# Opening layer 1 with four streams of q and k, and the last row of layer 0 by halves of channels

## The chip, the cores and the metric

The kernel runs on one core of one Trainium2 chip. The metric is the device time of one execution in microseconds (us). A core has five engines that run side by side, each through its own queue of instructions in order: PE (TensorE, matrix products), DVE (VectorE), ACT (ScalarE), POOL (GpSimd) and SP (SyncE, which here only issues transfers). They wait for one another by semaphores. PE writes its results into PSUM, which has eight banks; ACT and DVE bring them from there into SBUF, the working memory.

## The reference, cut to what matters

The input x has 128 rows of 256 positions with 256 channels. Two layers follow each other; each normalises over groups of channels, applies attention along each row and adds the input back.

```python
# layer 0: gated attention with 8 heads and a bias from pair_repr
x = x + _L0_conv_ref(_gn(x), ...)
# layer 1: banded attention with 4 heads
x = x + _L1_conv_ref(_gn(x), ..., 16)

def _gn(v, G=32, eps=1e-5):
    g = v.reshape(B_, H_, W_, G, C_ // G)
    m = jnp.mean(g, axis=(1, 2, 4), keepdims=True)
    s = jnp.var(g, axis=(1, 2, 4), keepdims=True)
    return ((g - m) / jnp.sqrt(s + eps)).reshape(v.shape)

def _L1_conv_ref(x, w_in, b_in, w_out, b_out, band):
    qkv = x2 @ w_in.T + b_in
    q, k, v = jnp.split(qkv, 3, axis=-1)          # 4 heads of 64
    scores = jnp.einsum('bhid,bhjd->bhij', q, k) / jnp.sqrt(D)
    scores = jnp.where(jnp.abs(i - j) <= band, scores, -jnp.inf)
    attn = jax.nn.softmax(scores, axis=-1)
    out = jnp.einsum('bhij,bhjd->bhid', attn, v)
    return out @ w_out.T + b_out
```

The statistics of `_gn` run over all rows. Layer 1 cannot begin before the last row of layer 0 has been added up and measured.

## The kernel before, in words

All data is float32. A row lies in SBUF with channels on the 128 partitions, in two halves of channels, and 256 positions along the free axis. Layer 1 works on pairs of rows: pair i has the rows 2i and 2i + 1, and there are 64 pairs. Between the layers the rows go through DRAM: layer 0 stores them with `settle` and its DMA at L1062, layer 1 loads them again with `load1` (L792, tiles `yg`).

The order of nearly all instructions is written out by hand (`tc.manual_schedule`), so on each engine they run in the order in which the Python code issues them. Layer 1 takes POOL into this order too; before it, and in what stands ahead of its `manual_schedule` block, POOL is placed by the framework.

*The end of layer 0.* `plain_output` is the output product of a row (32 matrix instructions in the trace, L587, tile `po`), `finish` (L1052) adds the row's input on DVE and `settle` (L1060) takes `bn_stats` of each half of channels. `settle_pair` does the same for the two rows of `o_last`. Then `channel_columns` joins the statistics: `bn_aggr` (L304), a product `ps_m` (L310), four small DVE instructions, a product `ps_v` (L319), a root on ACT (L322) and `rstd` (L324). Between these PE runs filler products with the tile `warm` (`keep_on`, L1261): five, two and three of them. `least` (L998) is a minimum that only a last test needs.

*Layer 1.* `normal(i)` normalises a pair into `1xn`, by DVE (L1309) or, for all pairs from 2 on, by ACT (L1307, with `shift` from L1554), and POOL forms three sums of it (`row_sums`, L579 to L581, tile `1ts`). q, k and the output are each a `Summed` stream: a 2x2 product done with seven products in place of eight, in the order 2, 1, 5, 6, 7, 4, 3. They accumulate in one PSUM bank, and after each the stream's half of the bank is taken out by ACT (2, 5, 6, 4) or DVE (1, 7, 3). `in_turn` runs several streams side by side, product by product. `values(s)` is v of one row (L1346, tile `p1v`, copied by ACT at L1353); `scores(s)` is the banded q k (L1367), the exp on ACT (L1375), and on POOL the mask (L1377, tile `1p`) and a sum (L1384). `attend(i)` is the weighted sum over v (L1408, tile `1av`) and the sums of weights (L1420, `1zs`). Their reciprocals `rz` (L1445) go out to DRAM and come back spread over the partitions (`by_transfer`, L1453 and L1457, tile `near`), and `divide` (L1477) reads `1av` and writes `1at`, which the output stream `1o` takes.

PSUM in layer 1: a ring of four banks serves streams, values and scores; `1av` and `1zs` have two banks each and one buffer. The loop over pairs in the steady state is: scores of pair i, `finish(i - 3)`, `attend(i - 1)`, `sums`, a stretch of three streams (q and k of pair i + 1, output of pair i - 2), `normal(i + 2)`, `divide(i - 1)`, values of pair i + 1. In the first two stretches and in the third there is no output stream yet, so only two streams run side by side:

```python
normal(0, False)
for p in weights:
    nc.gpsimd.memset(p, 0.0)
values(0)
values(1)
normal(1, False)
nc.vector.scalar_tensor_tensor(shift1, mean1, -1.0, rstd1, op0=ALU.mult, op1=ALU.mult)
stretch(0, -1)
```

Of the kernel before, what the change touches and what calls it, by code (L numbers as in the profile page):

```python
# [9 lines left out]
F32 = mybir.dt.float32  # L10
AF = mybir.ActivationFunctionType
ALU = mybir.AluOpType
# [3 lines left out]
P = 128  # L16
R = 256
# [22 lines left out]
def conv_preact_kernel(  # L40
# [35 lines left out]
    def proj_bank(name):  # L76
        return bank("proj", name)
# [591 lines left out]
    class Summed(Seven):  # L669
# [2 lines left out]

        def __init__(self, pool, weights, x, t, name, tag, bias=None, y=None):
            self.weights, self.x, self.t, self.by_token, self.name = weights, x, t, False, name
            self.bias, self.y = bias, y
            self.to = pool.tile([P, 4, R], F32, tag=tag, name=name, bufs=1)
            self.mid = pool.tile([P, R], F32, tag=f"mid{tag}", name=f"mid{name}", bufs=1)

        def out(self, to, half, m, r):

# [89 lines left out]
    with ExitStack() as both:  # L772
# [22 lines left out]
        with ExitStack() as lay0:  # L795
# [280 lines left out]
            def settle_pair(i):  # L1076

                if i >= 0:
                    settle(2 * i, 2 * i % XG, 2 * i % XG + 1, i)


            with tc.manual_schedule(
# [166 lines left out]
                weighted(S - 1)  # L1249
                gated(S - 1)  # L1250
                plain_output(S - 2)
                settle_pair(last - 1)
                finish(S - 2)
                plain_output(S - 1)
                finish(S - 1)
                warm = proj_bank("warm")

                def keep_on(n):
# [1 line left out]
                    for _ in range(n):  # L1260
                        nc.tensor.matmul(warm[:, 0, :], lhsT=ident, rhs=out_sb[:, 0, :], start=True, stop=True)  # L1261
# [8 lines left out]
        with ExitStack() as lay:  # L1270
# [10 lines left out]
            nc.gpsimd.memset(place, 0.0)  # L1281
            for half in range(2):
                nc.gpsimd.memset(place[KB * half : KB * (half + 1), 16 * half : 16 * (half + 1)], 1.0)

            spread = att.tile([P, 2, 2, P], F32, name="spread", bufs=1)
            for half in range(2):
                for r in range(2):
                    nc.gpsimd.tensor_copy(  # L1288
                        spread[:, half, r].rearrange("p (j d) -> p j d", j=2),
                        ident[:, B * r + 16 * half :: D1].unsqueeze(2).to_broadcast([P, 2, D1]),  # L1290
                    )
            xns, tss = {}, {}

            shift1 = att.tile([P, 2], F32, name="shift1", bufs=1)
# [1 line left out]
            def normal(i, by_scalar):  # L1296

                if 2 * i >= S:
                    return
                load1(i + 1)  # L1300
                xns[i] = row.tile([P, 4, R], F32, tag="xn", name=f"1xn{i}", bufs=2)
                for r in range(2):
                    for half in range(2):
# [16 lines left out]

            ats, ats_t, outputs, last_ots = {}, {}, {}, {}

            def stretch(i, j, amid=lambda n: None):


                streams = [
                    Summed(row, quarters1[w], xns[i], tss[i], f"1{w}{i}", w, bias=bqk[:, 0:2] if w == "q" else None)
                    for w in "qk"
                ]
                f, g = streams  # L1330
# [3 lines left out]
                in_turn(streams, amid)  # L1334
                for r in range(2):
                    st[2 * i + r].update(q=f.to[:, 2 * r : 2 * r + 2, :], k=g.to[:, 2 * r : 2 * r + 2, :])

            def values(s):
                if s >= S:
                    return  # L1340
                i, r = divmod(s, 2)
                ps = proj_bank(f"p1v{s}").rearrange("p a (b c) -> p (a b) c", c=P)
                for b in range(NB):
                    for kt in range(2):
                        for half in range(2):
                            nc.tensor.matmul(  # L1346
                                ps[KB * half : KB * (half + 1), b, :],
                                lhsT=xns[i][:, 2 * r + kt, KB * b : KB * (b + 1)],
                                rhs=w_in_t[:, kt, 2 * C + P * half : 2 * C + P * (half + 1)],
                                start=(kt == 0), stop=(kt == 1),  # L1350
                            )
                v = row.tile([P, NB, P], F32, tag="v", name=f"1v{s}")
                nc.scalar.copy(v, ps)  # L1353
                st[s]["v"] = v

            def scores(s, engine=nc.gpsimd):
                q, k = st[s]["q"], st[s]["k"]
# [186 lines left out]
            with tc.manual_schedule(engines={  # L1544
                mybir.EngineType.PE, mybir.EngineType.Activation, mybir.EngineType.DVE, mybir.EngineType.Pool,
                mybir.EngineType.SP,
            }):
                normal(0, False)
# [5 lines left out]
                nc.vector.scalar_tensor_tensor(shift1, mean1, -1.0, rstd1, op0=ALU.mult, op1=ALU.mult)  # L1554
                stretch(0, -1)
                last = S // 2 - 1
                for i in range(last):
                    s = 2 * i
                    scores(s)
                    scores(s + 1)  # L1560
                    finish(i - 3)
                    attend(i - 1)
                    sums(i - 1)
                    inverse(i - 1, 0)

                    def amid(n):
# [12 lines left out]
                    values(s + 3)  # L1579

                def all_of(s):
                    for _ in project(s):
# [241 lines left out]
```

## Time and profile before

| what | us |
|---|---|
| median of 3 runs | 3093.72 |
| lowest and highest run | 3090.98 and 3093.94 |
| the profiled execution, its own time | 3092.16 |
| span of the profiled execution, first to last instruction | 3090.2 |
| last row's output product begins on PE | 2012.46 |
| first product of layer 1 on PE | 2020.01 |
| third pair's streams begin (`1xn` of pair 2) | 2049.86 |
| first stretch with three streams begins | 2065.39 |

Times inside the execution count from the start of its span. The mean granted clock of PE was 0.993. A line of a timeline has the start, the length, the engine, the line of the kernel, the operation, what it writes and reads, its shape and how many were merged; in brackets stands how long the engine was idle before it and what ended that. Matrix instructions are pipelined, so their lengths overlap; prices are therefore taken from start to start.

### The profile page before, as it was taken

Reading aid. Unit: us, or ns where it says so; the run is one execution under the profiler, and the core shown is the slowest. Engines: PE = TensorE matmul, PEld = TensorE weight load, DVE = VectorE, ACT = ScalarE, POOL = GpSimd, SP = SyncE. Lnnn points to the kernel's source line nnn. Section 1 sums busy time; section 2 is a strip of 40 time slices with the busy share of each in tenths; the row PEclk is TensorE's granted clock in tenths of the full one; section 3 lists DMA queues with packets and bytes.
Section 4 is the critical chain, followed back from the end, with each engine's and each line's share of the span. In section 5 each row is a group of like instructions: output and inputs, shape, how many; then the busy total and the mean of one; then the engine's idle time right before and its main releaser. Section 6 shows DMA issues by size and latency. Waiting matters only on the chain.

```text
span 3090.2 us, 142498 instructions
## 1 busy us (share of the span) xinstructions
PE 3004.1 (97%) x62701; PEld 2061.0 (67%) x62701; DVE 2251.8 (73%) x4506; ACT 1911.6 (62%) x4323; POOL 1903.1 (62%) x1913
## 2 busy tenths in 40 slices
PE   6879999999999999999999999999999999999997
PEld 4546666666666666666666666667777777777775
DVE  4677788778877877787878787746666666666665
ACT  4656666666666666666666666645555555555553
POOL 3045656566666666666666665566777667777674
PEclk9999999999999999999999999999999999999999
DMA  9942222222222222222222222224444444444443
GB/s 378 423 136 53 53 65 62 57 56 65 62 57 56 65 62 53 60 65 62 52 62 65 62 52 61 65 57 100 103 97 100 104 99 98 98 105 98 99 97 71
DMA packets 385413, 280.84 MB, mean 91 GB/s; under 512 B 285104, under 2 KB 354192, under 8 KB 378640
## 3 DMA queue, kind: packets, MB, share of 16 engines
q1 hardware_dynamic: 383888, 269.27, 33.1%
q8 instruction: 494, 8.09, 1.1%
q0 software_dynamic: 752, 2.36, 0.2%
q14 instruction: 135, 1.11, 0.1%
q10 hardware_dynamic: 144, 0.00, 0.0%
HBM read 202.38 MB, written 69.17 MB: 88 GB/s over the span
## 4 chain that ended last, share of the span: by engine, by line
PE 91%; DMA 4%; DVE 2%; POOL 1%; ACT 0%; issue 0%; SPq 0%; DVEq 0%; POOLq 0%; ACTq 0%
PE sim L836 9%; PE av L868 7%; PE p1v L1346 7%; PE p1q L587 7%; PE po L587 6%; PE pbv L932 6%; PE p1k L587 6%; PE p1o L587 6%; PE pv L587 6%; PE pq L587 6%; PE pk L587 5%; PE pg L587 5%; PE zs L881 4%; DMA pr<-in_L_conv_pair_repr_dram 4%; PE 1sim L1367 3%; PE 1av L1408 3%
## 5 line engine op out<-in xcount | busy, mean ns | idle before, releaser
L849 ACT ACTIVATE ex<-sim 128x512 f32<-128x512 f32 x1024 | 555.2, 606 | 253.1 <-PE sim L836 253.1
L858 DVE TENSOR_TENSOR both<-ex 128x512 f32<-128x512 f32 x508 | 445.8, 897 | 63.6 <-ACT ex L849 63.4
L631 POOL TENSOR_TENSOR v<-v,midv 128x512 f32<-128x512 f32 x64 | 82.1, 1283 | 453.7 <-ACT v L625 453.7
L836 PE MATMUL sim<-q,k 32*64 32x256 f32 x8192 | 289.4, 388 | 1.3 <-ACT ex L849 1.3
L961 DVE RECIPROCAL rz<-zs 128x256 f32<-128x256 f32 x128 | 225.0, 1758 | 67.8 <-PE zs L881 52.4
L868 PE MATMUL av<-ex,v 128*32 128x256 f32 x4096 | 244.6, 379 | 1.6 <-DVE at L1026 1.6
L691 ACT ACTIVATE 1q<-p1q,bqk 128x256 f32<-128x256 f32 x192 | 90.9, 473 | 240.7 <-PE p1q L587 122.4
L1377 POOL TENSOR_TENSOR 1p<-1ex,seen 128x768 f32<-128x768 f32 x127 | 231.4, 1822 | 11.8 <-ACT 1ex L1375 11.8
L1346 PE MATMUL p1v<-w_in_t,1xn 128*64 128x128 f32 x4096 | 236.3, 273 | 0.2 <-POOL spread L1288 0.2
L1346 PEld LDWEIGHTS p1v<-w_in_t,1xn 128*64 128x64 f32 x4096 | 231.5, 137 | 6.1 <-POOL place L1281 0.6
L579 POOL TENSOR_TENSOR 1ts<-1xn 128x512 f32<-128x512 f32 x64 | 81.4, 1272 | 239.0 <-ACT 1xn L1307 239.0
L836 PEld LDWEIGHTS sim<-q,k 32*64 32x64 f32 x8192 | 152.1, 131 | 113.6 <-issue 66.6
L631 POOL TENSOR_TENSOR q<-q,midq 128x512 f32<-128x512 f32 x64 | 82.0, 1282 | 195.4 <-ACT q L625 195.4
L868 PEld LDWEIGHTS av<-ex,v 128*32 128x32 f32 x4096 | 131.9, 110 | 78.8 <-DVE at L1026 2.1
L1477 DVE TENSOR_TENSOR 1at<-1av,1near 128x512 f32<-128x512 f32 x128 | 82.5, 686 | 128.0 <-DMA 1near<-rz_far 106.8
L1384 POOL TENSOR_TENSOR 1zp<-1p 128x512 f32<-128x512 f32 x127 | 162.3, 1278 | 10.0
L1353 ACT COPY 1v<-p1v 128x512 f32<-128x512 f32 x128 | 75.0, 586 | 125.0 <-PE p1v L1346 125.0
L343 DVE BATCH_NORM_STATS2 stats<-xs 128x6 f32<-128x128 f32 x512 | 100.2, 274 | 64.4 <-DMA xs<-in_x_dram 64.4
L881 PE MATMUL zs<-both,place 128*32 128x256 f32 x2032 | 137.5, 387 | 0.5 <-DVE both L858 0.5
L1025 DVE TENSOR_TENSOR av<-av,bv 128x512 f32<-128x512 f32 x125 | 87.4, 699 | 62.7 <-ACT bv L954 60.4
L1445 DVE RECIPROCAL 1rz<-1z 128x64 f32<-128x64 f32 (+1 forms) x192 | 129.8, 678 | 2.2
L685 DVE SCALAR_TENSOR_TENSOR 1o<-p1o,bo_v,yg 128x256 f32<-128x256 f32 x183 | 88.6, 484 | 56.4 <-PE p1o L587 53.7
(353 smaller groups left out, 8351.3 us busy)
## 6 DMA issues: line engine op xcount, KB each, us to landing
pr<-in_L_conv_pair_repr_dram SPq DMA_DIRECT2D x32, 1024.0 KB
xs<-in_x_dram SPq DMA_DIRECT2D x16, 2048.0 KB
yg<-x SPq DMA_DIRECT2D x64, 512.0 KB
out_dram<-1o SPq DMA_DIRECT2D x256, 128.0 KB
xg<-in_x_dram SPq DMA_DIRECT2D x252, 128.0 KB
x<-o SPq DMA_DIRECT2D x63, 512.0 KB
near<-rz_far SPq DMA_DIRECT2D x500, 64.0 KB
1near<-rz_far SPq DMA_DIRECT2D x124, 256.0 KB
```

Source lines behind the costliest of these rows:

```text
L587: nc.tensor.matmul(out[cols], lhsT=lhsT[:, cols], rhs=rhs, **flags)
L631: nc.gpsimd.tensor_tensor(self.to[:, 2:4], self.to[:, 2:4], self.mid, ALU.add)
L836: nc.tensor.matmul(sims[j][KB * c : KB * (c + 1), kt, :], lhsT=k[p0 : p0 + D0, 2 * r + half, k0 : k0 + KB], rhs=q[p0 : p0 + D0, 2 * r + ha ...
L849: nc.scalar.activation(ex[:, j], sims[j], AF.Exp, scale=1.0 / math.sqrt(D0))
L858: engine.tensor_tensor(both[:, j : j + 2], ex[:, j : j + 2, 0, :], ex[:, j : j + 2, 1, :], ALU.add)
L868: nc.tensor.matmul(to[D0 * j : D0 * (j + 1), half, :], lhsT=v[:, 2 * r + half, c0 : c0 + D0], rhs=weights(4 * half + j, kt), start=(kt == ...
L881: nc.tensor.matmul(zs[strip(j), 0, :], lhsT=place0[:, half, :], rhs=both[:, j, :], start=(half == 0), stop=(half == 1),)
L932: nc.tensor.matmul(ps[strip(j), acc, half, :], lhsT=stationary[n][:, half, strip(j)], rhs=bias_of[n][:, 4 * half + j, :], start=(n <= 2 an ...
L961: nc.vector.reciprocal(rz, zs[:, 0, :])
L1346: nc.tensor.matmul(ps[KB * half : KB * (half + 1), b, :], lhsT=xns[i][:, 2 * r + kt, KB * b : KB * (b + 1)], rhs=w_in_t[:, kt, 2 * C + P * ...
L1377: engine.tensor_tensor(p.rearrange("p j (r c) -> p (j r) c", c=WROW)[:, :, 0 : 2 * WSTEP] .rearrange("p r (t c) -> p r t c", c=WSTEP)[:, : ...
L1384: engine.tensor_tensor(zp, p[:, :, 0:R], p[:, :, R : 2 * R], ALU.add)
```

## The change

It touches the last row of layer 0 and the first three stretches of layer 1. The work done is the same.

- The statistics of the two rows of `o_last` (`settle_pair(last - 1)`) are issued before the last row is weighted and gated, not after it.
- The last row's output product is written into two banks, one for each half of channels, and the input is added and measured half by half. Its store is issued here.
- `least(S - 1)` is issued inside `channel_columns`, ahead of the copy of `mean`.
- `shift` is formed directly after `rstd`. Pair 0 is normalised by DVE, pair 1 by ACT; the second half of the channels comes first. The memsets of the weights, `place` and `spread` are issued on POOL after both pairs' row sums (`fill`).
- q and k of pairs 0 and 1 run as four streams in one `in_turn`. Pair 1's streams write into the tags of `out` and `at`, their intermediate tiles into `z` and `rz`.
- Then come the scores of rows 0 and 1, the values of rows 0 and 1, `normal(2)`, the values of rows 2 and 3, the scores of rows 2 and 3 and `attend(0)`. In the stretch of pair 2 the values of rows 4 and 5 are placed between its products, in eight pieces. From the stretch of pair 3 on the order is that of before.

```diff
-    def in_turn(sevens, amid=lambda n: None):
+    def in_turn(sevens, amid=lambda n: None, between=iter(())):
         for p in sevens:
             p.open()
             p.product(2, p.ps[:, 1, :], first=True)
             p.take(2)
+        next(between, None)
         for n in (1, 5, 6, 7, 4, 3):
             for p in sevens:
                 p.product(n)
                 p.take(n)
             if n in (1, 5):
                 amid(n)
+            next(between, None)
+        for _ in between:
+            pass
...
                 products(av, S - 1, lambda h, kt: ex1[:, h % 4, kt, :], range(1, 2))
+                settle_pair(last - 1)
                 keep_av(S - 1)
...
                 plain_output(S - 2)
-                settle_pair(last - 1)
                 finish(S - 2)
-                plain_output(S - 1)
-                finish(S - 1)
+                po = {}
+                for m in range(2):
+                    po[m] = proj_bank(f"po{S - 1}_{m}")
+                    for kt in range(2):
+                        in_columns(
+                            po[m][:, m, :], out_sb[:, kt, m * P : (m + 1) * P], st[S - 1]["at"][:, kt, :], B,
+                            start=(kt == 0), stop=(kt == 1),
+                        )
+                o = outs[last]
+                for m in range(2):
+                    nc.vector.tensor_tensor(o[:, 1, m, :], po[m][:, m, :], st[S - 1]["xt"][:, m, :], ALU.add)
+                    nc.vector.bn_stats(out=stats1[:, m, most1.entry(last + 1), :], in_=o[:, 1, m, :])
+                nc.sync.dma_start(out=rows(x1, last * XG, XG), in_=o)
...
-                mean1, rstd1 = channel_columns(st1, most1, 1, keep_on)
-                least(S - 1)
+                def meanwhile(n):
+                    if n == 5:
+                        least(S - 1)
+                    keep_on(n)
+
+                mean1, rstd1 = channel_columns(st1, most1, 1, meanwhile)
...
+            def fill():
+                for p in weights:
+                    nc.gpsimd.memset(p, 0.0)
+                nc.gpsimd.memset(place, 0.0)
...
-                for half in range(2):
+                for half in (1, 0):
                     x, y = xns[i][:, 2 * r + half, :], ygs[i][:, r, half, :]
...
+            def projections(i, first=False):
+                tags = {"q": "out", "k": "at"} if first else {"q": "q", "k": "k"}
                 streams = [
...
+                    Summed(
+                        row, quarters1[w], xns[i], tss[i], f"1{w}{i}", tags[w], bias=bqk[:, 0:2] if w == "q" else None,
+                        bufs=2 if tags[w] == "at" else 1,
+                        mid=att.tile([P, R], F32, tag=("z", "rz")["qk".index(w)], name=f"mid1{w}{i}") if first else None,
+                    )
                     for w in "qk"
                 ]
...
-                normal(0, False)
-                for p in weights:
-                    nc.gpsimd.memset(p, 0.0)
-                values(0)
-                values(1)
-                normal(1, False)
                 nc.vector.scalar_tensor_tensor(shift1, mean1, -1.0, rstd1, op0=ALU.mult, op1=ALU.mult)
-                stretch(0, -1)
+                normal(0, False)
+                normal(1, True)
+                fill()
+                in_turn(projections(0) + projections(1, True))
                 last = S // 2 - 1
                 for i in range(last):
                     s = 2 * i
                     scores(s)
                     scores(s + 1)
+                    if i == 0:
+                        for _ in all_values(range(2)):
+                            pass
+                        normal(i + 2, True)
+                        for _ in all_values(range(2, 4)):
+                            pass
+                        continue
...
-                    stretch(i + 1, i - 2, amid)
+                    stretch(i + 1, i - 2, amid, all_values(range(s + 2, s + 4)) if i == 1 else iter(()))
...
-                    values(s + 2)
-                    values(s + 3)
+                    if i > 1:
+                        for _ in all_values(range(s + 2, s + 4)):
+                            pass
```

`values` became a generator that yields after each quarter of a row, and `all_values` runs through the rows it is given.

More of the change, by code (lines that the diff above doesn't have):

```diff
@@ L671, in conv_preact_kernel, with __init__ @@
         WIDTH = D1
-        def __init__(self, pool, weights, x, t, name, tag, bias=None, y=None):
+        def __init__(self, pool, weights, x, t, name, tag, bias=None, y=None, bufs=1, mid=None):
             self.weights, self.x, self.t, self.by_token, self.name = weights, x, t, False, name
             self.bias, self.y = bias, y
-            self.to = pool.tile([P, 4, R], F32, tag=tag, name=name, bufs=1)
-            self.mid = pool.tile([P, R], F32, tag=f"mid{tag}", name=f"mid{name}", bufs=1)
+            self.to = pool.tile([P, 4, R], F32, tag=tag, name=name, bufs=bufs)
+            self.mid = mid or pool.tile([P, R], F32, tag=f"mid{tag}", name=f"mid{name}", bufs=1)
         def out(self, to, half, m, r):
@@ L1280, in conv_preact_kernel @@
             place = att.tile([P, B], F32, name="place", bufs=1)
-            nc.gpsimd.memset(place, 0.0)
-            for half in range(2):
-                nc.gpsimd.memset(place[KB * half : KB * (half + 1), 16 * half : 16 * (half + 1)], 1.0)
             spread = att.tile([P, 2, 2, P], F32, name="spread", bufs=1)
[L1286 to L1291, printed above, removed]
+            def fill():
+                for p in weights:
+                    nc.gpsimd.memset(p, 0.0)
+                nc.gpsimd.memset(place, 0.0)
+                for half in range(2):
+                    nc.gpsimd.memset(place[KB * half : KB * (half + 1), 16 * half : 16 * (half + 1)], 1.0)
+                for half in range(2):
+                    for r in range(2):
+                        nc.gpsimd.tensor_copy(
+                            spread[:, half, r].rearrange("p (j d) -> p j d", j=2),
+                            ident[:, B * r + 16 * half :: D1].unsqueeze(2).to_broadcast([P, 2, D1]),
+                        )
             xns, tss = {}, {}
@@ L1302, in normal @@
                 for r in range(2):
-                    for half in range(2):
+                    for half in (1, 0):
                         x, y = xns[i][:, 2 * r + half, :], ygs[i][:, r, half, :]
@@ L1321, in conv_preact_kernel, with stretch @@
             ats, ats_t, outputs, last_ots = {}, {}, {}, {}
-            def stretch(i, j, amid=lambda n: None):
+            def projections(i, first=False):
+                tags = {"q": "out", "k": "at"} if first else {"q": "q", "k": "k"}
                 streams = [
-                    Summed(row, quarters1[w], xns[i], tss[i], f"1{w}{i}", w, bias=bqk[:, 0:2] if w == "q" else None)
+                    Summed(
+                        row, quarters1[w], xns[i], tss[i], f"1{w}{i}", tags[w], bias=bqk[:, 0:2] if w == "q" else None,
+                        bufs=2 if tags[w] == "at" else 1,
+                        mid=att.tile([P, R], F32, tag=("z", "rz")["qk".index(w)], name=f"mid1{w}{i}") if first else None,
+                    )
                     for w in "qk"
                 ]
-                f, g = streams
+                for r in range(2):
+                    st[2 * i + r].update({w: p.to[:, 2 * r : 2 * r + 2, :] for w, p in zip("qk", streams)})
+                return streams
+            def stretch(i, j, amid=lambda n: None, between=iter(())):
+                streams = projections(i)
                 if j >= 0:
@@ L1333, in stretch @@
                     streams.append(outputs[j])
-                in_turn(streams, amid)
-                for r in range(2):
-                    st[2 * i + r].update(q=f.to[:, 2 * r : 2 * r + 2, :], k=g.to[:, 2 * r : 2 * r + 2, :])
+                in_turn(streams, amid, between)
             def values(s):
@@ L1351, in values @@
                             )
+                    if b < NB - 1:
+                        yield
                 v = row.tile([P, NB, P], F32, tag="v", name=f"1v{s}")
@@ L1354, in values, with all_values @@
                 st[s]["v"] = v
+                yield
+            def all_values(rows):
+                for s in rows:
+                    yield from values(s)
             def scores(s, engine=nc.gpsimd):
@@ L1547, in conv_preact_kernel @@
             }):
+                nc.vector.scalar_tensor_tensor(shift1, mean1, -1.0, rstd1, op0=ALU.mult, op1=ALU.mult)
                 normal(0, False)
-                for p in weights:
-                    nc.gpsimd.memset(p, 0.0)
-                values(0)
-                values(1)
-                normal(1, False)
-                nc.vector.scalar_tensor_tensor(shift1, mean1, -1.0, rstd1, op0=ALU.mult, op1=ALU.mult)
-                stretch(0, -1)
+                normal(1, True)
+                fill()
+                in_turn(projections(0) + projections(1, True))
                 last = S // 2 - 1
```

## The prediction

> **What bounds the kernel now.** I read the page first, then the busy time by stretches, then the timelines of PE, DVE and POOL between 2009 and 2066 us, where the change lies, last the waits. The page puts PE at 97% of the span:
>
> ```profile
> PE 3004.1 (97%) x62701; PEld 2061.0 (67%) x62701; DVE 2251.8 (73%) x4506; ACT 1911.6 (62%) x4323; POOL 1903.1 (62%) x1913
> ```
>
> Busy time by stretch (length, then PE, PEld, DVE, ACT, POOL, clock) shows where PE is not full: only in the opening of layer 1, 2020 to 2066. From 2066 on it is busy all the time, so what the opening saves should reach the end.
>
> ```profile
> 2020.00:2034.00 14.00, 12.80 (x188) 8.66 (x188) 5.49 (x13) 6.36 (x14) 11.14 (x15) 1.00 0.22 74
> 2034.00:2050.00 16.00, 14.23 (x266) 9.94 (x264) 2.45 (x6) 8.60 (x21) 10.40 (x8) 1.00 0.01 3
> 2050.00:2066.00 16.00, 14.86 (x270) 10.29 (x270) 6.41 (x13) 9.14 (x22) 10.42 (x11) 1.00 0.26 69
> 2100.00:2300.00 200.00, 200.00 (x3562) 151.08 (x3560) 133.57 (x299) 107.74 (x259) 143.03 (x123) 1.00 0.42 98
> ```
>
> The PE timeline (start, length, what, idle before and its releaser) shows why: with two streams each product waits for the eviction of its stream's last one.
>
> ```profile
> 2014.33 2.42 PE L1261 MATMUL warm<-out_sb,ident 128*128 128x256 f32 x10
> 2016.76 0.36 PE L310 MATMUL ps_m<-mv,within 128*128 128x2 f32 x2
> ...
> 2018.26 1.54 PE L1261 MATMUL warm<-out_sb,ident 128*128 128x256 f32 x6
> 2020.01 3.71 PE L1346 MATMUL p1v<-w_in_t,1xn 128*64 128x128 f32 x64 [0.21 <-POOL spread L1288]
> ...
> 2026.12 0.65 PE L587 MATMUL p1q<-1ts,sums_1q 128*64 128x256 f32 x4 [0.26 <-DVE 1q L698]
> ...
> 2035.20 0.65 PE L587 MATMUL p1q<-1xn,w_in_t 128*64 128x256 f32 x4 [0.42 <-ACT 1q L691]
> ...
> 2063.46 1.41 PE L1408 MATMUL 1av<-1p,1v 64*64 64x80 f32 x63
> 2064.80 0.66 PE L1420 MATMUL 1zs<-1zp,place 64*32 64x256 f32 x16
> 2065.39 0.65 PE L587 MATMUL p1q<-1xn,w_in_t 128*64 128x256 f32 x4
> ```
>
> DVE's timeline holds three things used below: the end of the statistics, a small instruction stretched beside POOL, and the division that waits for a transfer. POOL's line shows its neighbour.
>
> ```profile
> 2016.19 0.42 DVE L304 BATCH_NORM_AGGREGATE mv<-stats 128x2 f32<-128x30 f32 x2
> 2021.71 1.23 DVE L1554 SCALAR_TENSOR_TENSOR shift<-mean,rstd 128x2 f32<-128x2 f32 x1
> 2060.92 1.29 DVE L1477 TENSOR_TENSOR 1at<-1av,1near 128x512 f32<-128x512 f32 x2 [1.78 <-DMA 1near<-rz_far]
> ```
> ```profile
> 2021.59 1.33 POOL L579 TENSOR_TENSOR 1ts<-1xn 128x512 f32<-128x512 f32 x1
> ```
>
> PE's waits from 2066 to 3030 (sum, times, longest) hold next to nothing:
>
> ```profile
> PE 1av L1408 <- issue: 0.6, 1, 0.6
> PE 1av L1408 <- DVE 1at L1477: 0.3, 1, 0.3
> ```
>
> **The Trainium skill.** "PSUM — Partial Sum Buffer", section "PSUM bank collisions raise a hardware error", has PSUM guarded by bank and quadrant, not by address. The trace agrees: product 1 writes the other half of its bank than the eviction of product 2 reads, and still waits (0.42 at 2035.20). "SBUF — State Buffer", section "Who interferes with whom": a DVE instruction with two SBUF inputs is blocked by a POOL instruction that reads SBUF. `shift` ends at 2022.94, POOL's 1ts at 2022.92: it agrees. "DMA: Bandwidth & Descriptors", section "Anatomy of one DMA", gives a transfer a fixed cost of about 2 us, mostly completion. The `near` way is two in a row; rz to division took 6.94 us for the first pair, more than two fixed costs.
>
> **Prices, start to start, unstalled.** A product of a stream 0.436 us (21 from 2065.39 to 2074.55), two rows of values 3.56 (3.52 to 3.59), two rows of scores 1.44 to 1.49, an `attend` 1.93 (2063.46 to 2065.39). From 2020.01 to 2065.39 are 45.38 us. The work in it: 42 products 18.31, six rows of values 10.7, six of scores 4.37, two attends 3.86, 37.24 in all. So 8.14 us are gaps: 2.58, 3.09 and 2.47 in the three two-stream stretches. This is all that the opening can win. The changed order has the same products, values and scores in it.
>
> **Part 1, the last row of layer 0.** The two `bn_stats` of `o_last` (1.28) move into DVE's idle 1.76 us before 2010.10: 2008.33 to 2009.6, and delay nothing queued behind; their input is ready at 2006.13. Their store is on SP before the last one either way. `o` of row S-2 then starts at 2012.24 instead of 2013.43. The first half of row S-1 is on PE by 2013.4, its add (0.42) and `bn_stats` (0.37) end by 2014.45, the second's by 2015.3, the aggregates by 2015.75, against 2016.61. That is 0.86 earlier on DVE. I count it as 0: PE's five fillers still run from 2014.33 to 2016.75, and `ps_m` is queued behind them; it started at 2016.76. The fillers are the cover; without them 0.86 would be gained. Below nothing there is no reason to go: `least` (0.40), now ahead of `mean`, fits into DVE's wait for `ps_m` (0.54, and the 0.86). After `rstd` (2018.90), `shift` is now ahead of 1xn: about 0.1 with POOL idle, where the 1.23 would need a POOL neighbour that is not there. But `least` no longer is, so 1xn starts near 2019.05. PE is free of the last fillers at 2019.74; first product then, instead of 2020.01: **-0.27**. The last store of x leaves 0.5 earlier; its landing (2018.6 before, when SP could issue the next load) is awaited by the first products too and stays hidden. SP's order of transfers is unchanged.
>
> **Part 2, four streams.** 28 products, 12.21 us; a round of four is 1.74, more than the 1.23 from product to product seen through an eviction (2049.86 to 2051.09), so the old waits go. New ones: ACT first does four 1xn of pair 1 (pitch 0.495, from 2019.14 to 2021.12), so the first eviction ends at 2021.6 where PE is ready at 2021.48: **+0.18**, with 16 evictions queued behind. Four take ACT 1.27 (pitches 0.36 and 0.27 when not waiting), so it catches up. POOL does pair 0's row sums from 2020.5 (2.81), pair 1's first sum ends at 2024.6; product 5 of pair 1 is due at 2024.25: **+0.40** (0 to 0.8). Its next sums come 1 us ahead of need. The memsets of 1p, `place` and `spread` (4.26 + 2.1) move behind them and end at 2032.5, before the first use at 2034.3. Streams end at 2019.74 + 12.21 + 0.58 = 2032.53.
>
> **Part 3, up to the third stretch.** Scores 0 and 1: 1.49. Values 0 to 3: 7.1, on banks freed by each exp (pitch 0.41) in time. Scores 2 and 3: 1.45 and **+0.14**, since 1v3's copy stands behind the 1xn of pair 2 on ACT and frees the last bank late. Attend 0: 1.93. So stretch 2 starts at 2044.64 instead of 2049.86.
>
> **Part 4, values in the gaps of stretch 2.** 14 products and 8 pieces of 0.44: 9.66, a round 1.30, over 1.23, so no wait: 2054.30. Before, stretch and values took 12.16. Scores: to 2055.74.
>
> **What is late next.** Attend 1 writes the bank that division 0 reads. Division 0 is 4.19 (rz; 4.12 before) + transfers + 1.29 + 0.08 after the stretch's start. Transfers were 6.94 here and 6.4 to 7.0 in the six pairs that follow; I take their mean, 6.74. That gives 2056.94, so attend 1 waits **+1.20** (0.85 to 1.40), all of PE behind it. Before, the division was done at 2062.21 and attend began at 2063.46: the slack is used up. ACT runs 1v5, 1xn, then 1ex of scores 4 and 5, to 2059; PE needs those banks about then, so an earlier transfer would give 0.3 at most.
>
> Sum: third pair's streams start at 2056.94 + 1.93 = 2058.87 instead of 2065.39: **-6.5** (8.14 + 0.27 - 0.18 - 0.40 - 0.14 - 1.20). After it the order is as before. The profiled execution was 3092.16 (span 3090.2 and 1.96 around it), which would become 3085.7, span 3083.7. The median of the runs stands 1.56 above it: 3093.72 - 6.5 = 3087.2.
>
> **Rivals.** (a) The opening stays ragged: ACT or POOL hold each of seven rounds by one product's slot, 3.0 us, gain 3.5, 3090.2. For it: ACT has evictions, 1xn and exps in one queue, and is the one that starts late; against: 16 evictions at 0.32 are 5.1 of 12.2 us. Within the bound. (b) More comes: fillers do not hold `ps_m` (+0.86), or `near` lands early (+0.3): gain up to 7.7, 3086.0. Against it: the filler's end and `ps_m`'s start coincide. (c) Slower: the pairs after the opening settle where each attend waits for its division. Place: 1av behind 1at, about 60 times. DVE waits for `near` there in most pairs, and the division ends only 0.7 to 1.3 before 1av. Past 0.7 later every pair pays; 1.1 later is 0.4 x 60 = 24, so 3111; it decides from about 0.8 (6 us). Against: order and queues of those pairs are unchanged, and PE waited once, 0.3. (d) The halves do not do what they are for: that is the forecast for part 1.
>
> **Numbers.** About 0.2% (6.2 us) is what a measurement of this kernel can tell from no change, and the forecast stands just past it. Forecast 0.62 (0.47 of it past the bound), (b) 0.13, (a) 0.17, (c) 0.08. So faster 0.60, same 0.32, slower 0.08. The range takes in (b), (a) and 1.5 us of spread between runs: 3084.3 to 3092.3.
>
> **What would show it.** `ps_m` 2.4 us after the fillers' start, with DVE idle about 1.0 before `mean`; 28 products in 12.8 us with one POOL wait; one PE wait of about 1.2 for 1at at the second 1av. Wrong if PE waits for ACT in several rounds, if that 1av waits nothing, or if waits for 1at repeat after 2070.

## The result, and the profile after

The changed kernel took 3087.45 us (median of 13 runs, 3084.23 to 3088.84), the kernel before 3093.12 in the same comparison (13 runs). The ratio is 0.9981 with a 95% interval of 0.9972 to 0.9989. A second comparison gave 3087.32 (11 runs) against 3093.78 (24 runs): 0.9977, 0.9968 to 0.9986. So it is faster, by 5.7 and 6.5 us in the two pairs of medians. Whether that lies beyond 0.2% is not settled, since both intervals contain 0.998. The profiled execution took 3088.84 at a mean PE clock of 0.993.

The page, its span and its engines:

```profile
span 3086.7 us, 142499 instructions
...
PE 3004.4 (97%) x62701; PEld 2062.4 (67%) x62701; DVE 2248.5 (73%) x4503; ACT 1913.6 (62%) x4327; POOL 1901.1 (62%) x1913
```

PE's sum is what it was, with 3.5 us less span around it. Where it went is seen in the busy time by stretch of the opening (length, then PE, PEld, DVE, ACT, POOL, clock, DMA share, GB/s):

```profile
2022.00:2036.00 14.00, 13.78 (x173) 9.19 (x173) 5.18 (x13) 9.03 (x22) 10.90 (x17) 1.00 0.20 70
2036.00:2052.00 16.00, 16.00 (x350) 14.20 (x344) 3.10 (x6) 9.62 (x22) 14.94 (x11) 1.00 0.01 3
2052.00:2068.00 16.00, 14.82 (x266) 11.03 (x264) 8.85 (x19) 8.81 (x22) 8.30 (x8) 1.00 0.28 69
```

The middle stretch, where PE had 14.23 of 16, is now full. The last one keeps its gap. PE's timeline names what is left:

```profile
2014.51 1.93 PE L587 MATMUL po<-at,out_sb 128*32 128x256 f32 x32 [0.61 <-DVE at L1030]
2016.38 2.43 PE L1276 MATMUL warm<-out_sb,ident 128*128 128x256 f32 x10
2018.64 0.28 PE L310 MATMUL ps_m<-mv,within 128*128 128x2 f32 x2
...
2020.06 1.54 PE L1276 MATMUL warm<-out_sb,ident 128*128 128x256 f32 x6
2021.81 0.65 PE L587 MATMUL p1q<-1xn,w_in_t 128*64 128x256 f32 x4 [0.21 <-ACT 1xn L1333]
...
2023.56 0.63 PE L587 MATMUL p1q<-1xn,w_in_t 128*64 128x256 f32 x4
...
2026.58 0.65 PE L587 MATMUL p1q<-1ts,sums_1q 128*64 128x256 f32 x4 [0.23 <-POOL 1ts L579]
...
2034.50 1.80 PE L1409 MATMUL 1sim<-1q,1k 64*64 64x96 f32 x64
...
2046.74 0.65 PE L587 MATMUL p1q<-1xn,w_in_t 128*64 128x256 f32 x4
...
2059.38 1.44 PE L1450 MATMUL 1av<-1p,1v 64*64 64x80 f32 x64 [1.18 <-DVE 1at L1519]
2060.75 0.66 PE L1462 MATMUL 1zs<-1zp,place 64*32 64x256 f32 x16
2061.34 0.65 PE L587 MATMUL p1q<-1xn,w_in_t 128*64 128x256 f32 x4
```

Two brackets remain between 2022 and 2061: POOL's row sums, and the second `1av`, which waits for the first pair's division. DVE's timeline shows why that division is late, and that `shift`, with POOL idle, took 0.16 where it had taken 1.23:

```profile
2017.31 0.42 DVE L304 BATCH_NORM_AGGREGATE mv<-stats 128x2 f32<-128x30 f32 x2
2017.64 0.36 DVE L1002 TENSOR_REDUCE zmin<-z 128x1 f32<-128x256 f32 x1
2018.96 0.16 DVE L312 COPY mean<-ps_m 128x2 f32<-128x2 f32 x1 [0.95 <-PE ps_m L310]
...
2020.73 0.16 DVE L1590 SCALAR_TENSOR_TENSOR shift<-mean,rstd 128x2 f32<-128x2 f32 x1
...
2049.58 1.36 DVE L1487 RECIPROCAL 1rz<-1z 128x128 f32<-128x128 f32 x2
...
2057.94 1.29 DVE L1519 TENSOR_TENSOR 1at<-1av,1near 128x512 f32<-128x512 f32 x2 [1.70 <-DMA 1near<-rz_far]
```

From `rz`'s end (2050.94) to the division (2057.94) are 7.00 us.

**Why the span fell by 3.5 and the opening by 6.1.** R is the start of the last row's output product, 2012.46 before and 2014.51 after. From R to the first stretch with three streams were 52.93 us, and are now 46.83. Layer 0 ran 2.05 later in the execution after. It was late from its start, which nothing in the change touches. The first scores on PE, before and then after:

```profile
229.69 1.12 PE L836 MATMUL sim<-q,k 32*64 32x256 f32 x32
```
```profile
231.80 1.12 PE L840 MATMUL sim<-q,k 32*64 32x256 f32 x32
```

The rest of layer 1 took 0.55 more, -6.10 + 2.05 + 0.55 = -3.5; in a second profile of the changed kernel, taken later, it took 0.42 less than before, with R at 2016.03. So single executions differ by as much as the terms in dispute, and the experiments are read from R on PE. Their single times are given, but do not decide.

After the opening, PE's waits between 2062 and 3030 (sum, times, longest) stay small: no pair waits for its division in turn.

```profile
PE 1av L1450 <- issue: 1.6, 3, 0.6
...
PE 1av L1450 <- DVE 1at L1519: 0.4, 2, 0.2
```

### The profile page after: what moved, and what is told of

Its sections match the earlier page's. It is cut to its first block, busy times and chain, and to the rows that moved or that the text cites. A ratio compares the mean times of both kernels' runs of the same rounds, so it can differ in the third digit from the quotient of the medians.

```text
span 3086.7 us, 142499 instructions
## 1 busy us (share of the span) xinstructions
PE 3004.4 (97%) x62701; PEld 2062.4 (67%) x62701; DVE 2248.5 (73%) x4503; ACT 1913.6 (62%) x4327; POOL 1901.1 (62%) x1913
## 4 chain that ended last, share of the span: by engine, by line
PE 91%; DMA 5%; DVE 2%; POOL 1%; issue 0%; ACT 0%; SPq 0%; DVEq 0%; POOLq 0%; ACTq 0%
PE sim L840 9%; PE av L872 7%; PE p1v L1380 7%; PE p1q L587 6%; PE pbv L936 6%; PE po L587 6%; PE p1k L587 6%; PE p1o L587 6%; PE pq L587 6%; PE pv L587 6%; PE pk L587 5%; PE pg L587 5%; PE zs L885 4%; PE 1sim L1409 3%; DMA pr<-in_L_conv_pair_repr_dram 3%; PE 1av L1450 3%
## 5 line engine op out<-in xcount | busy, mean ns | idle before, releaser
L1333 ACT ACTIVATE 1xn<-yg,shift,rstd 128x256 f32<-128x256 f32 x252 | 130.7, 591 | 0.6 <-DVE shift L1590 0.6
```

## The experiments

"Opening" is the time from R to the first stretch with three streams; "to values" goes on to the values behind that stretch, which shows waits that only come inside it. All in us from R.

| kernel | first layer-1 product | stretch of pair 2 | opening | to values |
|---|---|---|---|---|
| before | 7.55 | 37.40 | 52.93 | 62.09 |
| after | 7.30 | 32.23 | 46.83 | 55.99 |
| last row only | 7.30 | 39.90 | 55.44 | 64.60 |
| last row only, memsets behind | 7.30 | 36.80 | 52.33 | 61.49 |
| opening only | 7.58 | 32.57 | 46.70 | 55.86 |
| values behind the stretch | 7.30 | 32.23 | 47.82 | 56.98 |
| two by two | 7.31 | 37.23 | 51.38 | 60.54 |
| attend 0 first | 7.30 | 32.38 | 45.90 | 55.61 |
| no transfer | 7.30 | 32.25 | 45.56 | 55.27 |
| fewer fillers | 6.33 | 31.56 | 46.26 | 55.42 |
| attend first, 1xn spread | 7.30 | 32.39 | 45.78 | 54.94 |
| all three | 6.33 | 31.68 | 45.08 | 54.24 |
| changed again | 7.31 | 32.25 | 46.28 | 55.44 |

**One part alone: the last row.** The kernel before, with the edits of layer 0's end and the place of `least`; the opening as before.

```diff
+                settle_pair(last - 1)
                 keep_av(S - 1)
...
-                settle_pair(last - 1)
                 finish(S - 2)
-                plain_output(S - 1)
-                finish(S - 1)
+                po = {}
+                for m in range(2):
...
-                least(S - 1)
+                def meanwhile(n):
```

> The kernel before with part 1 alone: the last row's output in two banks, residual and statistics by halves, settle_pair and least moved; the opening of layer 1 as before. Measure: the opening's length on PE, from the start of the last row's output product to the start of the first stretch with three streams; 52.93 before, 46.83 after. Theory (PE's five fillers hold ps_m): DVE ends its aggregates about 0.9 earlier, ps_m follows the start of the fillers by 2.26 as in the changed kernel and not 2.43, so 52.7. Rival (the statistics chain was the path): ps_m 0.86 earlier, so 52.1.

Both missed. The opening grew to 55.44, 2.5 longer than before; the run took 3098.52, beside 3097.39 for the kernel before. PE's timeline shows the last row doing what was forecast (first product at 7.30 from R), then one large hole, and behind it products that start 0.88 apart, where 0.43 to 0.48 is usual:

```profile
2020.22 0.28 PE L310 MATMUL ps_m<-mv,within 128*128 128x2 f32 x2
...
2031.66 1.12 PE L587 MATMUL p1q<-1ts,sums_1q 128*64 128x256 f32 x4 [2.41 <-DVE 1q L698]
2032.54 1.09 PE L587 MATMUL p1k<-1ts,sums_1k 128*64 128x256 f32 x4
```

The busy times of this stretch have the granted clock at 0.50, and not at 1.00:

```profile
2031.60:2034.40 2.80, 2.74 (x14) 1.46 (x16) 0.24 (x1) 0.85 (x2) 2.30 (x3) 0.50 0.00 0
```

DVE was behind with that eviction, above all because of one instruction in its queue. The view of its `1xn` tiles of both pairs gives the least, median and longest length in ns, and the start of the first and the last:

```profile
L1326 DVE TENSOR_SCALAR 1xn<-yg,mean,rstd x8: 407/410/5081, 2022.3 to 2026.0; 128x256 f32<-128x256 f32 x8
```

The last one ran from 2026.03 to 2031.11; the two ahead of it took 1.37 and 0.88. POOL's timeline has the neighbour:

```profile
2021.89 0.12 POOL L1298 MEMSET place<- 128x32 f32 x1 [12.15 <-PE ps_v L319]
...
2026.04 0.72 POOL L581 TENSOR_TENSOR 1ts<-1xn,1ts 128x256 f32<-128x256 f32 x1
2026.70 4.26 POOL L1567 MEMSET 1p<- 128x1216 f32 x4
```

The four memsets end at 2030.96. In the kernel before, `place` waited for `least` (13.37 <-DVE zmin at 2019.49), and started 0.36 behind DVE's first `1xn`; here it starts 0.43 ahead of it. So with `least` moved ahead POOL's work comes earlier against DVE's, and the memsets fall on pair 1's `1xn`. That is a reading of two timelines. The next run tests what the memsets did; that `least` is what released `place` sooner was not tested.

**The memsets moved.** As the last one, with the memsets of `1p` issued on POOL behind pair 1's row sums.

```diff
                 normal(0, False)
-                for p in weights:
-                    nc.gpsimd.memset(p, 0.0)
                 values(0)
                 values(1)
                 normal(1, False)
+                for p in weights:
+                    nc.gpsimd.memset(p, 0.0)
```

> The kernel before with part 1, as in the first experiment, and one thing more: POOL's four memsets of 1p are issued behind the row sums of pair 1 and not ahead of them. There the opening was 55.43 and not 52.7, with one 1xn of pair 1 on DVE lasting 5.08 until POOL's memsets were done. Theory (DVE's instruction is shut out while POOL works, and the memsets held it): the 1xn of pair 1 end within 0.5 of POOL's row sums of pair 0, the wait of 2.41 at a product of the first stretch is gone, and the opening is 52.5 to 53.0. Rival (halves in two banks, or an order on DVE, cost it): still 55.

The opening took 52.33, 3.1 less than with the memsets in their old place, 0.6 less than before, and a little less than was expected. (The one execution, 3098.31 beside 3092.49, started its last row 3.4 later than the profiled kernel before and took 3.2 longer behind the opening; why is not known.) The hole is gone:

```profile
2029.26 0.65 PE L587 MATMUL p1q<-1ts,sums_1q 128*64 128x256 f32 x4 [0.26 <-DVE 1q L698]
```

So the memsets beside a DVE instruction were the cause. Of the 3.1 us, 2.15 are the hole itself (2.41 against 0.26) and 0.94 the four products behind it at half the clock. In the changed kernel `fill` stands behind both pairs' sums, and ACT normalises pair 1.

**The other part alone: the opening.** The changed kernel with layer 0's end as before (`settle_pair`, `finish` and `least` in their old places).

> The changed kernel with part 1 undone: last row, settle_pair and least as before, the opening of layer 1 as changed. Theory: the opening gives all but 0.2 of the gain, so its length on PE is 47.0 to 47.1 (52.93 before, 46.83 after). Rival (the halves carry a good part): 47.7.

46.70, against 46.83 with both parts, and less than the 47.0 expected; the run took 3087.88. PE's timeline:

```profile
2018.54 0.35 PE L310 MATMUL ps_m<-mv,within 128*128 128x2 f32 x2
...
2058.98 1.44 PE L1433 MATMUL 1av<-1p,1v 64*64 64x80 f32 x64 [0.71 <-DVE 1at L1502]
```

`ps_m` came 4.29 after R, not 4.13, and the stretch of pair 2 0.34 later. The shorter wait for the division gave that back: the transfers took 6.53 here, 7.00 there. Up to the stretch of pair 2, where no transfer counts yet, part 1 is worth 0.34 of the 5.17 gained; the rest is the opening's.

**Values behind the stretch again.**

```diff
-                    stretch(i + 1, i - 2, amid, all_values(range(s + 2, s + 4)) if i == 1 else iter(()))
+                    stretch(i + 1, i - 2, amid, iter(()))
...
-                    if i > 1:
+                    if i > 0:
```

> The changed kernel with part 4 undone: in the stretch of pair 2 nothing is placed between its products, and the values of rows 4 and 5 come behind it, as before. The stretch then has its waits back (8.6 and 3.56 against 9.77). Theory (attend 1 is held by division 0, whose transfers are out 12.5 after the stretch's start): the wait at the second 1av vanishes, attend 1 begins 13.6 after the stretch's start and not 12.64, so the opening is 0.9 longer, 47.8. Rival (the gaps' filling is worth all of its 2.4): 49.2.

47.82 (run 3087.3), as expected: 1.0 more. Two streams wait for evictions again, and the `1av` follows the scores at once:

```profile
2050.61 0.65 PE L587 MATMUL p1q<-1ts,sums_1q 128*64 128x256 f32 x4 [0.22 <-ACT 1q L691]
...
2060.40 1.39 PE L1450 MATMUL 1av<-1p,1v 64*64 64x96 f32 x62
```

With the wait of 1.43 (start to start) taken off, the changed kernel would have 45.40. So the placed values fill 2.4 us of gaps, and the wait for the division takes 1.4 back.

**Two streams and two, in place of four.**

```diff
-                in_turn(projections(0) + projections(1, True))
+                in_turn(projections(0))
+                in_turn(projections(1, True))
```

> The changed kernel with the four streams run two and two: first q and k of pair 0, then those of pair 1; all else as changed. Theory (a round of four covers an eviction, a round of two doesn't): the streams take two times 8.6 and not 12.69, the opening is 4.5 longer, 51.3. Rival (the gain comes from the new order of values and scores): 1 to 2 longer, 48 to 49.

The stretch of pair 2 starts 5.0 later, and after a shorter wait for the division the opening is 51.38 (run 3092.95), as the theory had it and 4.55 more than with four streams. Three quarters of the opening's gain come from this line. The gaps return, to ACT and DVE in turn:

```profile
2023.95 0.65 PE L587 MATMUL p1q<-1xn,w_in_t 128*64 128x256 f32 x4 [0.65 <-ACT 1q L691]
...
2033.80 0.65 PE L587 MATMUL p1q<-1ts,sums_1q 128*64 128x256 f32 x4 [0.26 <-DVE 1q L698]
...
2064.33 1.44 PE L1450 MATMUL 1av<-1p,1v 64*64 64x80 f32 x64 [0.74 <-DVE 1at L1519]
```

**No transfer for the first pair.** What is late behind the division?

```diff
-                        if n == 5:
+                        if n == 5 and i == 1:
+                            nc.gpsimd.memset(hd["z", 0][2], 1.0)
+                        elif n == 5:
                             by_transfer(i - 1)
```

> The changed kernel where near of pair 0 is set to ones by POOL instead of being carried out and back; the division of pair 0 by its sums is left out by this. Theory now (ACT's queue is late right behind the transfers): the wait at the second 1av goes, the first evictions of the next stretch wait, and up to the values behind that stretch it takes 55.3 to 55.5 (55.99 after). The prediction's words were 0.3 at most, 55.7. Rival (nothing else held PE): 54.6.

**Attend 0 ahead of the scores of rows 2 and 3.** Another way to take the wait away, with the computation whole: `rz` and its transfers start sooner.

```diff
+                    if i == 1:
+                        attend(0)
+                        sums(0)
+                        for part in range(3):
+                            inverse(0, part)
+                        by_transfer(0)
                     scores(s)
                     scores(s + 1)
...
```

Further down the edit takes the same steps for pair 0 out of their old place.

> The changed kernel with attend 0, its sums, all three parts of rz and the transfers issued ahead of the scores of rows 2 and 3, so that division 0 is some 2.5 earlier against PE. Measure to a later point too: from the start of the last row's output product to the values behind the first stretch with three streams, 62.09 before and 55.99 after. Theory now: the wait at the second 1av (1.2) goes, but ACT's queue (1v5, four 1xn of pair 3, exps of rows 4 and 5, then the first evictions of that stretch) is late next, so 55.5 to 55.7. Rival (the transfers alone held PE): 54.7 to 54.8. If nothing was held there: 56.0.

In both the second `1av` waits for nothing, and the openings, 45.56 and 45.90, are 1.3 and 0.9 shorter. But inside the next stretch PE stops for ACT, so that to the values only 0.72 and 0.38 are left (runs 3082.98 and 3087.87). Against the changed kernel's second profile, 55.44, where the transfers were shorter, it is 0.17 and nothing. PE without the transfer, and with attend 0 first:

```profile
2060.12 0.65 PE L587 MATMUL p1q<-1xn,w_in_t 128*64 128x256 f32 x4 [0.26 <-ACT 1q L691]
```
```profile
2063.86 0.65 PE L587 MATMUL p1q<-1xn,w_in_t 128*64 128x256 f32 x4 [0.26 <-ACT 1q L691]
```

ACT's timeline of the latter shows its queue: from the copy of `1v5`, the values of row 5, on it has no pause, and the first eviction of the stretch comes last.

```profile
2058.70 0.59 ACT L1389 COPY 1v<-p1v 128x512 f32<-128x512 f32 x1 [1.85 <-PE p1v L1380]
2059.19 2.08 ACT L1333 ACTIVATE 1xn<-yg,shift,rstd 128x256 f32<-128x256 f32 x4
...
2061.57 1.60 ACT L1417 ACTIVATE 1ex<-1sim 128x384 f32<-128x384 f32 x4
...
2063.30 0.51 ACT L691 ACTIVATE 1q<-p1q,bqk 128x256 f32<-128x256 f32 x1
```

**Attend 0 first, and ACT's 1xn of pair 3 spread.** The same, with the four `1xn` instructions placed between the values' pieces, where ACT had paused 1.85. `gaps` runs through the values like `all_values` and issues the `1xn` in between.

```diff
...
-                    stretch(i + 1, i - 2, amid, all_values(range(s + 2, s + 4)) if i == 1 else iter(()))
-                    normal(i + 2, True)
+                    stretch(i + 1, i - 2, amid, gaps(range(s + 2, s + 4), 3) if i == 1 else iter(()))
+                    if i != 1:
+                        normal(i + 2, True)
...
```

> Attend 0 and its transfers issued ahead, and besides the four 1xn of pair 3 placed on ACT between the evictions of the stretch of pair 2, and not behind the copy of 1v5. Theory (behind the transfers it was ACT's queue that was late): no wait is left at the second 1av nor at the first evictions of the stretch with three streams; up to the values behind that stretch 54.8 to 55.0 (55.99 after, 55.61 with the attend ahead alone). Rival (the 1xn delay the evictions among which they stand, or POOL's sums are late): 55.4 or more.

54.94 to the values (run 3087.49), 0.67 less than without the spreading. Between the copy and the exps ACT's queue now holds only 0.6 us of other work (`1same`):

```profile
2058.66 0.58 ACT L1413 COPY 1v<-p1v 128x512 f32<-128x512 f32 x1 [1.36 <-PE p1v L1404]
...
2059.56 1.62 ACT L1441 ACTIVATE 1ex<-1sim 128x384 f32<-128x384 f32 x4
```

Of PE's waits between 2018 and 2080 two are left, at the start of the opening:

```profile
PE p1q L587 <- POOL 1ts L579: 0.2, 1, 0.2
PE p1q L587 <- ACT 1xn L1333: 0.2, 1, 0.2
```

**Fewer fillers.** Was it the fillers that held `ps_m`?

```diff
-        wait(5)
+        wait(3)
...
-        wait(3)
+        wait(2)
...
-                    if n == 5:
+                    if n == 3:
```

> The changed kernel with fewer of PE's filler products: three and not five ahead of ps_m, two and not three behind ps_v. Theory (the fillers hold ps_m, so that what the halves gain on DVE is lost): ps_m 0.75 earlier, 3.4 behind the start of the last row's output product and not 4.13; the last 0.43 is given back, since the first evictions wait for ACT's 1xn. Up to the values behind the first stretch with three streams 55.1 to 55.2 (55.99 after). Rival (fillers cost nothing, or the clock falls without them): 56.0 or more.

Yes. `ps_m` came 3.36 after R, 0.77 sooner, now 0.15 behind the end of DVE's aggregates, and the clock of this stretch stayed at 1.00 (run 3087.82). The first product came 0.97 sooner; at the stretch of pair 2 0.67 of that was left, since the evictions wait for ACT's `1xn` of pair 1. To the values it was 55.42, more than the 55.1 to 55.2 expected: the transfers took 7.10 in this execution. DVE and PE:

```profile
2016.34 0.42 DVE L304 BATCH_NORM_AGGREGATE mv<-stats 128x2 f32<-128x30 f32 x2
```
```profile
2015.41 1.56 PE L1276 MATMUL warm<-out_sb,ident 128*128 128x256 f32 x6
2016.91 0.35 PE L310 MATMUL ps_m<-mv,within 128*128 128x2 f32 x2
...
2019.88 0.65 PE L587 MATMUL p1q<-1xn,w_in_t 128*64 128x256 f32 x4 [0.36 <-PE warm L1276]
```

**All three, beside the changed kernel again.** Attend first, 1xn spread and fewer fillers together.

> The same with fewer fillers (three ahead of ps_m, two behind ps_v), a candidate that should beat both kernels. Theory: the gains add, 0.6 to 0.7 for the fillers and 1.1 for the rest, so 54.1 to 54.3 up to the values behind the first stretch with three streams, against 55.99 after and 62.09 before: about 1.8 us less than the changed kernel and 7.9 less than the kernel before, a ratio of 0.9974. Rival (another queue is late when PE comes earlier): 54.8 or more.

> The changed kernel once more, beside the candidate and the kernel before on one chip. Its opening should again take 55.99 up to the values behind the first stretch with three streams, give or take the 0.3 by which the transfers of pair 0 differ, and its ratio to the kernel before be 0.998, that is 6 us; the candidate should be 1.8 below it, which the runs' spread may hide.

To the values the opening took 54.24, 1.75 less than the changed kernel's 55.99 and 7.85 less than before, and 1.20 less than the changed kernel's second profile (55.44, which is further from 55.99 than the 0.3 allowed for). In the runs it was 3086.38 (15 runs, 3081.91 to 3090.95) against 3087.32 for the changed kernel on the same chip; the ratios to the kernel before are 0.9977 (0.9969 to 0.9985) and 0.9977 (0.9968 to 0.9986). The traces, one of each kernel and two of the changed one, show the gain; the runs can't tell it apart. The changed kernel's second profile also shows the transfers' spread: they took 6.44 in it, and the wait for the division halved.

```profile
2060.35 1.44 PE L1450 MATMUL 1av<-1p,1v 64*64 64x80 f32 x64 [0.62 <-DVE 1at L1519]
```

## Why the prediction was right, and which terms were off

The forecast case came: 3087.2 against 3087.45 and 3087.32. That the absolute time fits to 0.25 is in part luck: the kernel before came out as 3093.12 and 3093.78 where the forecast had 3093.72, and the gains are 5.7 and 6.5 where it had 6.5. The opening's gain was forecast as 6.5 and is 6.10 in the first profile and 6.65 in the second. By its steps, in the first profile where nothing else is said:

- **PE is full after the opening, so the gain reaches the end.** It held: no new wait repeats after 2062. What hid it in the span was the 2.05 us of layer 0, and 0.55 behind the opening.
- **Part 1, 0 at `ps_m`.** Right for the changed kernel, misread for the kernel before. Behind the fillers `ps_m` can start 2.26 after they start, as it does after the change. Before, it started at 2016.76, 2.43 after them, but 0.15 after the end of DVE's aggregates (2016.61), the same 0.15 as with fewer fillers. So before it was DVE's chain that held it; the fillers would have let it go 0.17 earlier. Of some 0.94 that the halves gain on DVE, 0.17 came through (`ps_m` at 4.13 after R instead of 4.30), and taking fillers away released the other 0.77. `least` fitted into DVE's wait, and `shift` took 0.16.
- **First product, -0.27.** It measured 7.30 after R, forecast 7.28. This hides two errors: `ps_m` was 0.17 early, and PE started 0.21 after the last filler where I had let it start at once.
- **Four streams, 12.79.** 12.69. POOL's wait was sized as 0.40 and was 0.40 (product due at about 2026.18, started at 2026.58). ACT's 0.18 did not come: the first eviction ended at 2023.49, and product 1, which needs that bank, began at 2023.56 without a wait.
- **Scores and values.** Scores 0 and 1 took 1.73, not 1.49; they wait for the last evictions' banks, which I had not counted (the last eviction ended at 2035.36, and the second row's products went on at 2035.41). The 0.14 at scores 2 and 3 did not come (1.44). The stretch of pair 2 began 32.23 after R, forecast 32.18.
- **Stretch of pair 2, 9.66.** 9.77, with no wait in it.
- **Wait for the division, 1.20 (0.85 to 1.40).** Start to start 1.43 in the first profile and 0.87 in the second; as idle time the traces name 1.18 and 0.62. The term that scatters is the transfer, taken as 6.74 from six pairs between 6.4 and 7.0; for the first pair, where its division waits for them, the kernels here gave 6.31 to 7.10. Two transfers in a row it is, but not two of one length. By the semaphores in the traces the two ways out landed 1.7 and 2.2 us after the end of `rz` in every run that has them, to within 0.02; the ways back were issued at once, and landed at 5.15 to 5.39 and at 6.21 to 7.01. So most of the time and nearly all of the scatter lie on the way back. What makes it scatter is open.
- **"An earlier transfer would give 0.3 at most".** Too low: without the transfer 0.72 was gained against the first profile, though only 0.17 against the second (55.44). That ACT's queue is late next was right, and spreading its `1xn` showed it.

Rival (a), a ragged opening, did not come: no stretch of the streams lost a slot each round. Rival (b) came in part: its 0.86 is there as 0.17, and as 0.77 more once fillers are taken away. Rival (d) is the forecast of part 1, and was right but for 0.17. Rival (c) needed the waits for `1at` to repeat; they sum to 0.4 in the 968 us behind.

What the prediction didn't see is that part 1 alone makes the opening longer. It named the release of `place` nowhere, and its sum for part 1 holds only with the memsets moved behind the row sums. The Trainium skill's "SBUF — State Buffer", "Who interferes with whom", which I had used for `shift`, speaks of this too: it counts `tensor_scalar` among the instructions that can take the ports shared with POOL, and says that whoever comes second blocks fully, for one instruction of the other. The trace agrees that DVE was blocked, and goes further: 5.08 us, over five POOL instructions in a row.

## What to carry to other kernels

Where two chains wait for each other's evictions, look for two more that are ready: here four streams in one round took out 4.55 us with the same instructions. Then ask what is late next, and next again; here it was the division's transfer, then ACT's queue, and each time part of the wait removed came back at the next place. And before an instruction is moved, list who waits for it on other engines: POOL's work that starts sooner can come to lie beside a DVE instruction that had been clear of it. Last, when two things end close together ahead of a third, ask by how much each holds it: the aggregates and the fillers were 0.17 us apart.

## What the runs showed of the hardware

- A DVE `TENSOR_SCALAR` of 128x256 takes 0.41 us. With the last row alone changed, three of eight were stretched beside POOL: 1.37 and 0.88 us beside its first two row sums, and 5.08 beside the third and four memsets in a row. Each ended 0.15 after POOL's work beside it. Behind each of the first two sums POOL paused for 0.08 us, and one of DVE's instructions came to its end; from the third sum to the last memset there was no pause. Moving the memsets removed the 5.08. The memsets read nothing from SBUF. In the kernel before, two DVE `TENSOR_TENSOR` with one input in PSUM (L698) took their usual 0.42 beside the same memsets.
- After PE's pause of 2.41 us there, its granted clock was 0.50 from 2031.6 to 2034.4, and products started 0.88 apart. The shorter pauses in the opening of the other runs left it at 1.00.
- With the five fillers cut to three, and the three to two, the granted clock behind them stayed at 1.00; PE's longest pause there was 0.36. A run without fillers is not among these.
- PE stood idle 0.21 us between the last filler and the first product of layer 1 in the kernel before and after. In the trace PE's queue has semaphore instructions there: after the last filler ended (2021.60 in the changed kernel) two of them ended, at 2021.65 and 2021.76, and the weights were loaded from 2021.78 on. With fewer fillers it was 0.36: DVE's first `1xn` ended after the last filler (2019.56, 2019.52), and three such instructions ended behind it. Which semaphore each was for is not shown.
